# An edge-gated graph layer on one core: edge sums in pairs two to three steps late, the add one step early, products of a block spread over its steps

## The chip, the core and the metric

The kernel runs on one core of a Trainium2 chip. The metric is the device time of one execution in microseconds (us). A core has TensorE (PE, with its weight loads PEld), VectorE (DVE), ScalarE (ACT), GpSimd (POOL) and SyncE (SP), which run side by side, each through its own queue in order, and 16 DMA engines that all queues share.

## The reference

A layer of a graph network over B = 16 batches, N = 1024 nodes and D = 256 features. `adj` is sparse: some 9 of 1024 entries in a column are not zero, and A_a = A_m = adj.

```
pre_u = einsum('bud,dk->buk', h_t, W1[:d])
pre_v = einsum('bvd,dk->bvk', h_t, W1[d:])
hidden = relu(pre_u[:, :, None, :] + pre_v[:, None, :, :] + b1)
S = sigmoid(einsum('buvk,ko->buvo', hidden, W2)[..., 0] + b2[0])
a_t = einsum('buv,bud->bvd', S * A_a, h_t)
m_t = einsum('uv,bud->bvd', A_m, h_t) * h_t
z_t = beta1 * h_t + beta2 * (einsum('bvd,de->bve', a_t, Wa) + ba) + beta3 * (einsum('bvd,de->bve', m_t, Wm) + bm)
```

## The kernel before

**Edges, not pairs.** The kernel makes a list of edges per 128 columns v of `adj` (`lists`, L239 to 373): the rows u of the nonzero entries and their values. Only where there is an edge does it work out the gate S. Nodes with more edges than a list holds are finished in a loop at the end (L842 on), none of whose instructions shows in the trace.

**Tables.** Batches are taken in 4 groups of GB = 4. Per group there is a table in DRAM with 1024 rows of 8 KB: pre_u of 4 batches, then h of 4 batches. `rows` (L434) makes the first half of 128 rows with TensorE (`half_product`, L425 to 428), ScalarE copies it out (tile `tab`, L443), SP stores it (L446); `copy_h` (L419) copies the second half from DRAM to DRAM, issued on ACT's queue in the main loop.

**Blocks and steps.** A block is (group, 128 nodes v); there are 32, in an order that takes node blocks 0 to 5 of groups 0 and 1 first, since lists are still being made. A block has T = 10 steps: two windows (w) of 64 nodes, of TW = 5 steps, each of 128 edges. A step n = 10k + s does this:

- `fetch` (L494) has GpSimd gather the 128 table rows of the step's edges into one of NF = 6 buffers `fetched`, about 0.94 MB. It is issued for step n - 1 + 6 once step n - 1 has been summed. `fetch_val` (L379) gathers edge values of new lists, two per step.
- `expand` (L564) has TensorE copy pre_v of each edge's node to its row: `pc` = mark x X, 128 x 1024 in PSUM (two buffers, pool `psc`). X is made by `halves` (L452) for the block after this one: products with w_v (L427), b1 by L431, copies by ScalarE (L461 to 468) and a subtraction by VectorE (`low`, L463).
- `gate` (L598) has VectorE add `fetched` and `pc` into the one tile `t` (L601), then make relu, the product with W2 and its sum for each of 4 batches (L606); ScalarE makes the sigmoid (L609) and scales the edge values by it (L612) into tile `left`, which `left_adj` (L573) has filled with the edge values for each batch (L579).
- `aggregate` (L614) has TensorE sum the edges of a node (L623): the stationary operand is a 128 x 32 piece of `left` (16 nodes, once with and once without gate), so that 4 batches lie side by side in 128 columns, in a half of an accumulator `acc0` or `acc1`. A step touches one quarter of the window (8 instructions in the trace) or two (16).
- `half_end` (L628) has ScalarE copy an accumulator to `ev0` or `ev1` (L631) when half a window is complete.

**Products of a block.** `turn_over` (L633) transposes `ev` on TensorE (L641), copies it by ScalarE into `LT` (L644), and some steps later VectorE multiplies the ungated half by h (`times_h`, L654). `block_end` (L659) then makes, in four pieces, the products with Wa and Wm (L672) and the bias (L431), copies them to tile `z` by ScalarE (L675), adds beta1 x h on VectorE (L676; h in `h_blk`, loaded by SP at L775) and stores z through SP (L678). Transposes, products, rows and halves share two PSUM buffers named `misc` (pool `psm`).

**What sets the order.** The order on each engine is written by hand (`manual_schedule`, L471): instructions are queued as the Python loop at L745 calls them. `after(step, f)` puts f off to `do(step)`, which stands behind `gate` of that step. `fill` puts one VectorE instruction of a list under way ahead of each gate product. `plan` (L726) says at which steps a block's x is loaded (first number) and its row products are made. Per step the queue order is:

```python
        if 1 <= n <= total:
            aggregate(n - 1)
            fetch_val(2)
            if n - 1 + NF < total:
                fetch(n - 1 + NF)
        ...
            gate(n)
            if n + 1 < total:
                left_adj(n + 1)
        ...
        do(n)
        if n + 2 < total:
            expand(n + 2)
```

Behind these come the block's pieces: `turn_over` at s = 1 (last quarter pair of the block before), 7 (two) and 9, `block_end` at s = 3 to 6, `halves` at s = 0, 2, 3, 5, 6.

## Time and profile before

| | us |
|---|---|
| runs of the kernel | 1163.63, 1163.78, 1171.99 |
| their median | 1163.78 |
| the profiled execution, first to last instruction (span) | 1165.8 |
| PE busy | 1092.1 (94%) |
| PEld busy | 723.1 (62%) |
| DVE busy | 1056.2 (91%) |
| ACT busy | 893.5 (77%) |
| POOL busy | 439.9 (38%) |
| bytes moved by DMA | 391.40 MB, mean 336 GB/s |
| of these the gathers' queue | 300.50 MB, 68.9% of the 16 engines' span |

The profile is that of one execution. The time of the profiled execution is known as its span alone. Ends of matmuls are modelled, since they are pipelined: starts are what to read on TensorE. A matmul in fp32 shows as two records, one in fp32r as one. On VectorE a gate product shows as the product and a short DVE_READ_ACCUMULATOR. A share of DMA is the mean share of time in which its 16 engines had a packet under way; packets overlap a little, so that it can pass 1. "A <- B" in a list of waits says that A's engine stood idle until B ended. Block k starts where I put the add (L601) of its step 0: 71.6 us for block 0, 309.4 for block 6, 513.2 for block 12, 897.6 for block 24, 1117.5 for block 31.

### The profile page before, as it was taken

How to read it: one execution, taken by the hardware profiler on the slowest of the kernel's cores; microseconds unless marked ns; L12 is line 12 of the kernel's file. 1: busy time of each engine (PE TensorE's matmuls, PEld its weight loads, DVE VectorE, ACT ScalarE, POOL GpSimd, SP SyncE). 2: the span in 40 equal slices, each digit the busy share in tenths (PEclk: the TensorE clock that was granted, in tenths of full speed). 3: DMA queues.
4: the chain of work that ended last, by engine and by line, in shares of the span. 5: the costliest groups of instructions: out<-in, count | busy, mean ns of one | idle time of the engine just before them, and what ended most of it. 6: DMA issues, size and time to landing. Idle time of an engine off the chain costs nothing. (4 is left out here: it accounts for less than half of the span.)

```text
span 1165.8 us, 23918 instructions
## 1 busy us (share of the span) xinstructions
PE 1092.1 (94%) x7633; PEld 723.1 (62%) x7633; DVE 1056.2 (91%) x3487; ACT 893.5 (77%) x2624; POOL 439.9 (38%) x428
## 2 busy tenths in 40 slices
PE   7867899999999999999999999999999999999986
PEld 6744666666666666666666666666666666666553
DVE  7688889888999989999999999999999999999994
ACT  2346587767887878888888888888888888888873
POOL 1556645253335333443333333333333333333330
PEclk9868899999999999999999999999999999999999
DMA  9986898999999999999999999999998998999991
GB/s 286 298 307 223 277 372 312 362 320 331 342 320 323 396 379 336 358 350 402 389 374 369 355 364 356 360 364 383 371 375 324 361 322 333 334 339 328 328 346 60
DMA packets 147048, 391.40 MB, mean 336 GB/s; under 512 B 16753, under 2 KB 105329, under 8 KB 110705
## 3 DMA queue, kind: packets, MB, share of 16 engines
q0 software_dynamic: 50016, 300.50, 68.9%
q1 hardware_dynamic: 81616, 74.99, 20.0%
q10 hardware_dynamic: 15280, 14.29, 3.7%
q8 instruction: 63, 1.03, 0.3%
q14 instruction: 73, 0.59, 0.1%
HBM read 393.78 MB, written 50.33 MB: 381 GB/s over the span
## 5 line engine op out<-in xcount | busy, mean ns | idle before, releaser
L496 POOL DMA_INDIRECT fetched<-table,uidx x320 | 341.5, 1067 | 628.3 <-PE acc L623 447.2
L606 DVE SCALAR_TENSOR_TENSOR t<-t,w_b 128x256 f32<-128x256 f32 x1280 | 478.3, 421 | 19.3 <-ACT left L612 0.5
L601 DVE TENSOR_TENSOR t<-fetched,pc 128x1024 f32<-128x1024 f32 x320 | 389.3, 1217 | 41.4 <-PE pc L569 13.9
L623 PE MATMUL acc<-fetched,left 128*32 128x256 f32 x4096 | 336.2, 391 | 31.9 <-ACT left L612 26.2
L612 ACT ACTIVATE left<-left,gt 128x32 f32<-128x32 f32 (+1 forms) x1280 | 299.3, 304 | 10.4
L569 PE MATMUL pc<-X,mark 128*128 128x512 f32 x640 | 237.6, 453 | 6.2 <-ACT mark L562 5.0
L623 PEld LDWEIGHTS acc<-fetched,left 128*32 128x32 f32 x4096 | 130.6, 109 | 179.3 <-issue 52.4
L569 PEld LDWEIGHTS pc<-X,mark 128*128 128x128 f32 x640 | 97.2, 191 | 140.0 <-issue 89.3
L609 ACT ACTIVATE gt<-sc,b_b 128x4 f32<-128x4 f32 x320 | 96.2, 301 | 43.4 <-DVE t L606 40.8
L672 PE MATMUL misc<-w_m,LT 128*128 128x256 f32 x496 | 117.2, 379 | 0.0
L672 PE MATMUL misc<-w_a,LT 128*128 128x256 f32 x496 | 117.1, 379 | 0.0
L579 ACT ACTIVATE left<-onehot,val 128x128 f32<-128x128 bf16 (+1 forms) x320 | 116.5, 364 | 0.0
L427 PE MATMUL misc<-w_v,hT 128*128 128x256 f32 x448 | 107.3, 383 | 0.0
L427 PE MATMUL misc<-w_u,hT 128*128 128x256 f32 x416 | 101.2, 390 | 5.7 <-ACT few L329 3.6
L606 DVE DVE_READ_ACCUMULATOR t<-t,w_b 128x1 f32 x1280 | 104.0, 81 | 0.0
L672 PEld LDWEIGHTS misc<-w_a,LT 128*128 128x128 f32 x496 | 93.9, 189 | 15.1
L672 PEld LDWEIGHTS misc<-w_m,LT 128*128 128x128 f32 x496 | 93.8, 189 | 14.9
L382 POOL DMA_INDIRECT val<-in_adjT_dram,vidx x80 | 85.7, 1071 | 35.1 <-issue 22.4
L427 PEld LDWEIGHTS misc<-w_v,hT 128*128 128x128 f32 x448 | 86.0, 192 | 13.9
L427 PEld LDWEIGHTS misc<-w_u,hT 128*128 128x128 f32 x416 | 79.5, 195 | 17.3 <-ACT few L329 3.7
L631 ACT COPY ev<-acc 128x512 f32<-128x512 f32 x128 | 75.5, 590 | 14.6 <-PE acc L623 4.2
L675 ACT COPY z<-misc 128x512 f32<-128x512 f32 x62 | 36.3, 586 | 58.1 <-PE misc L672 38.8
(164 smaller groups left out, 947.9 us busy)
## 6 DMA issues: line engine op xcount, KB each, us to landing
h_blk<-in_x_dram SPq DMA_DIRECT2D x31, 512.0 KB
out_dram<-z SPq DMA_DIRECT2D x31, 512.0 KB
hT<-in_xT_dram SPq DMA_DIRECT2D x28, 512.0 KB
table<-in_x_dram ACTq DMA_DIRECT2D x24, 512.0 KB
table<-tab SPq DMA_DIRECT2D x24, 512.0 KB
fetched<-table,uidx POOLq DMA_INDIRECT x320
table<-in_x_dram SPq DMA_DIRECT2D x8, 512.0 KB
table<-fetched SPq DMA_DIRECT2D x8, 512.0 KB
```

The costliest lines, as they stand in the source:

```text
L382: nc.gpsimd.indirect_dma_start(out=val[:, i, j:j + 1], out_offset=None, in_=adj_flat, in_offset=bass.IndirectOffsetOnAxis(ap=vidx[:, i, j: ...
L427: nc.tensor.matmul(p[:, bb * D:(bb + 1) * D], hT[:, 2 * h + bb, i, :], wt[:, i, :], start=(i == 0 and not begun), stop=(i == DC - 1), skip ...
L496: nc.gpsimd.indirect_dma_start(out=fetched[n % NF], out_offset=None, in_=table[g], in_offset=bass.IndirectOffsetOnAxis(ap=uidx[:, vt * NW ...
L569: nc.tensor.matmul(pcs[n][:, c], marks[n // TW][:, j * P:(j + 1) * P], cuts[k][:, w, c], start=True, stop=True)
L579: nc.scalar.activation(lefts[n][:, :m, :, 0, :], onehot[:, i, o:o + m, :].unsqueeze(2).to_broadcast([P, m, GB, V]), AF.Copy, scale=val[:, ...
L601: nc.vector.tensor_tensor(t, fetched[n % NF][:, :GD].rearrange("p (b d) -> p b d", b=GB), pcs.pop(n).rearrange("p (b d) -> p b d", b=GB), ...
L606: nc.vector.scalar_tensor_tensor(t[:, b, :], t[:, b, :], 0.0, w2_b, ALU.max, ALU.mult, accum_out=sc[:, b:b + 1])
L609: nc.scalar.activation(gt, sc, AF.Sigmoid, bias=b2_b)
L612: nc.scalar.activation(lefts[n][:, :m, b, 1, :], lefts[n][:, :m, b, 0, :], AF.Copy, scale=gt[:, b:b + 1])
L623: nc.tensor.matmul(accs[h][b * 2 * V:(b + 1) * 2 * V, r, :], left[:, i, b].rearrange("p k v -> p (k v)"), f[:, GD + b * D:GD + (b + 1) * D ...
L631: nc.scalar.copy(evs[q], accs.pop(q))
L672: nc.tensor.matmul(pz[:, bb * D:(bb + 1) * D], LTs[k][:, c, 2 * h + bb, i, :], wt[:, c, :], start=False, stop=(i == 0 and c == DC - 1), sk ...
```

## The change

- **Add one step ahead, in place.** `gate` is cut in two: `add(n)` puts fetched + pc into the gathered buffer itself (no tile `t`), and is called for step n + 1 ahead of `gate(n)`.
- **Edge sums in pairs.** `aggregate` is called at odd n alone, for steps n - 3 and n - 2, and in order at the very end. `left` has five buffers in place of three. It holds the ungated values once for two batches (7 slots of 16 in place of 8), so ScalarE's first copy into it is half as large.
- **Gather buffers.** 7 in place of 6, freed in order of use (`free`, `at_slot`), and an eighth from step 110, when the lists are done and their pool `lst` is closed. Gathers are issued as buffers come free, two at a time.
- **z without a tile of its own.** ScalarE copies the product into `LT`, whose transposed sums are used up; VectorE adds beta1 x h into `h_blk`, and the store leaves from `h_blk`. `LT` is laid out anew, and the transposes write `pt` in runs of 16.
- **Products spread.** `turn_over` at s = 0, 2, 8, 9; row products by new plans (groups 2 and 3 at s = 8 and 9, the last at step 219 where it was 233). Up to step 119 expand and products are queued ahead of the step's add and gate, from 120 on behind them as before.

```diff
+    lst = lst.enter_context(tc.tile_pool(name="lst", bufs=1))
...
-    NF = 6
+    NF = 7
+    at_slot, free = {}, list(range(NF))
...
     def fetch(n):
         k, g, vt, w, j = where(n)
+        at_slot[n] = free.pop(0)
         nc.gpsimd.indirect_dma_start(
-            out=fetched[n % NF], out_offset=None, in_=table[g],
+            out=fetched[at_slot[n]], out_offset=None, in_=table[g],
...
-        lefts[n] = wk.tile([P, 2, GB, 2, V], FP, name="left")
-        nc.scalar.activation(lefts[n][:, :m, :, 0, :], onehot[:, i, o:o + m, :].unsqueeze(2).to_broadcast([P, m, GB, V]),
+        lefts[n] = wk.tile([P, 2, 2 * GB - 1, V], FP, name="left", bufs=5)
+        nc.scalar.activation(lefts[n][:, :m, 1::GB, :],
+                             onehot[:, i, o:o + m, :].unsqueeze(2).to_broadcast([P, m, GB // 2, V]),
                              AF.Copy, scale=val[:, i, j:j + 1])
...
+    def add(n):
+        t = fetched[at_slot[n]][:, :GD]
+        nc.vector.tensor_tensor(t, t, pcs.pop(n), ALU.add)
+
     def gate(n):
-        k, g, vt, w, j = where(n)
-        t = one.tile([P, GB, D], FP, name="t")
-        nc.vector.tensor_tensor(t, fetched[n % NF][:, :GD].rearrange("p (b d) -> p b d", b=GB),
-                                pcs.pop(n).rearrange("p (b d) -> p b d", b=GB), ALU.add)
+        m = len(QUARTERS[n % TW])
+        t = fetched[at_slot[n]][:, :GD].rearrange("p (b d) -> p b d", b=GB)
...
-                                 left[:, i, b].rearrange("p k v -> p (k v)"), f[:, GD + b * D:GD + (b + 1) * D],
+                                 left[:, i, 2 * b - b % 2:2 * b - b % 2 + 2].rearrange("p k v -> p (k v)"), f[:, GD + b * D:GD + (b + 1) * D],
...
-            LTs[k] = one.tile([P, DC, GB, 2, P], FP, name="LT")
+            LTs[k] = one.tile([P, GB, 2, DC, P], FP, name="LT")
         LT = LTs[k]
-        pt = small("pt")
+        pt = small("pt").rearrange("p (r k c v) -> p r k c v", r=2, c=DC, v=V)
...
-            nc.tensor.transpose(pt[:, i * P:(i + 1) * P], ev[:, r, c * P:(c + 1) * P], ident)
+            nc.tensor.transpose(pt[:, r, :, c, :], ev[:, r, c * P:(c + 1) * P], ident)
...
-        after(step + (1 if k == BS - 1 else 2), times_h)
+        after(step + (1 if k == BS - 1 or w else 2), times_h)
...
-            nc.scalar.copy(z[:, sl], pz.rearrange("p (b d) -> p b d", b=2))
-            after(step + 2, lambda sl=sl: nc.vector.scalar_tensor_tensor(z[:, sl], hb[:, sl], be1, z[:, sl],
-                                                                         ALU.mult, ALU.add))
-        after(step + 3, lambda: nc.sync.dma_start(
-            out[g * GB:(g + 1) * GB, vt * P:(vt + 1) * P, :].rearrange("b p d -> p b d"), z))
+            z = LTs[k][:, 2 * h].rearrange("p k c n -> p (k c n)").rearrange("p (b d) -> p b d", b=2)
+            nc.scalar.copy(z, pz.rearrange("p (b d) -> p b d", b=2))
+            after(step + 1, lambda sl=sl, z=z: nc.vector.scalar_tensor_tensor(hb[:, sl], hb[:, sl], be1, z,
+                                                                              ALU.mult, ALU.add))
+        after(step + 2, lambda: nc.sync.dma_start(
+            out[g * GB:(g + 1) * GB, vt * P:(vt + 1) * P, :].rearrange("b p d -> p b d"), hb))
...
+    def products(n, k, s):
+        nonlocal end, parts, piece, last
+        if (s == 2 and 0 < k < BS) or n == total:
             turn_over(k - 1, 1, 1, n)
...
+        if s in (8, 9) and n < total - T:
+            turn_over(k, 0, s - 8, n)
...
+        if (s == 0 and 0 < k < BS) or n == total - 1:
+            turn_over(k - (s == 0), 1, 0, n)
...
+    ROOM, MORE = 110, 1
+    ahead = NF
+    add(0)
+
+    def refill():
+        nonlocal ahead
+        while free and ahead < total:
+            fetch(ahead)
+            ahead += 1
+
+    def gather_in(n):
+        aggregate(n)
+        free.append(at_slot.pop(n))
+        fetch_val(2)
+        refill()
+        if (n + 1) % TW in (0, MID + 1):
+            half_end(n, 0 if (n + 1) % TW else 1)
+
+    done = 0
+    for n in range(total + 2):
+        k, s = divmod(n, T)
+        if n < total - 3:
+            last_in = n - 1 if n % 2 else done
+        else:
+            last_in = n
+        while done < min(last_in, total):
+            gather_in(done)
+            done += 1
...
+        if n < 120:
+            if n + 2 < total:
+                expand(n + 2)
+            products(n, k, s)
+        if n + 1 < total:
+            add(n + 1)
+        if n < total:
+            gate(n)
+            if n + 1 < total:
+                left_adj(n + 1)
+        do(n)
+        if n >= 120 and n + 2 < total:
+            expand(n + 2)
...
+        if n >= 120:
+            products(n, k, s)
+        if n == ROOM:
+            assert not running and all(next(x, None) is None for x in made)
+            lists_done()
+            more = main.enter_context(tc.tile_pool(name="more", bufs=1))
+            for i in range(MORE):
+                free.append(len(fetched))
+                fetched.append(more.tile([P, 2 * GD], FP, name=f"fetched{len(fetched)}"))
+            refill()
```

## The prediction

> **What bounds the kernel now.** I read the view by stretches first, cut at the start of blocks 0, 6, 12, 24 and 31 (ten steps each, the last from 1117.5 us). Columns: stretch, its length, busy us of TensorE, weight loads, VectorE, ScalarE and GpSimd, granted clock, share of the DMA engines, GB/s.
>
> ```profile
> 71.00:309.00 238.00, 216.90 (x1423) 143.50 (x1422) 205.30 (x706) 168.93 (x492) 117.20 (x114) 0.94 0.89 312
> 309.00:513.00 204.00, 197.20 (x1400) 130.92 (x1401) 194.21 (x649) 165.08 (x487) 86.51 (x81) 1.00 0.96 352
> 513.00:898.00 385.00, 382.72 (x2767) 252.32 (x2766) 363.83 (x1145) 325.96 (x973) 131.25 (x122) 1.00 0.99 368
> 898.00:1117.00 219.00, 212.04 (x1529) 134.65 (x1527) 210.08 (x665) 184.73 (x557) 72.77 (x70) 1.00 0.92 335
> ```
>
> Three resources are close to full at once: TensorE 99%, VectorE 95% and DMA 0.99 from 513 to 898; VectorE 96% with DMA down to 0.92 afterwards. A share says little then; the timeline must show who never stands still. First VectorE in block 27, where no table rows are made any more:
>
> ```profile
> 1000.40 0.08 DVE L606 DVE_READ_ACCUMULATOR t<-t,w_b 128x1 f32 x1
> 1000.57 1.22 DVE L601 TENSOR_TENSOR t<-fetched,pc 128x1024 f32<-128x1024 f32 x1
> 1001.89 0.42 DVE L606 SCALAR_TENSOR_TENSOR t<-t,w_b 128x256 f32<-128x256 f32 x1
> ...
> 1003.28 0.69 DVE L654 TENSOR_TENSOR LT<-LT,hT 128x512 f32<-128x512 f32 x1
> 1003.88 1.21 DVE L601 TENSOR_TENSOR t<-fetched,pc 128x1024 f32<-128x1024 f32 x1
> 1005.13 0.42 DVE L606 SCALAR_TENSOR_TENSOR t<-t,w_b 128x256 f32<-128x256 f32 x1
> ```
>
> No other engine is waited for, yet VectorE loses time. The add starts 0.09 after the last gate instruction ends (1000.48 to 1000.57), and the first gate instruction starts 0.10 after the add ends (1001.79 to 1001.89): each needs what the one before it did to tile `t`. Where an unrelated instruction stands between (L654), add and product overlap by 0.08 (1003.97 against 1003.88). So a block is bound here by VectorE's own neighbours. It takes 31.29 us (add to add, 991.99 to 1023.28), and so does nearly every block from 24 to 30. Now TensorE in block 21:
>
> ```profile
> 801.35 1.07 PE L623 MATMUL acc<-fetched,left 128*32 128x256 f32 x16
> 802.35 0.73 PE L569 MATMUL pc<-X,mark 128*128 128x512 f32 x2
> 802.92 0.60 PE L641 MATMUL misc<-ident,ev 128*128 128x128 f32 x4
> 803.45 0.64 PE L623 MATMUL acc<-fetched,left 128*32 128x256 f32 x8
> 804.01 0.72 PE L569 MATMUL pc<-X,mark 128*128 128x512 f32 x2
> 804.58 0.39 PE L431 MATMUL misc<-b_p,unit 128*128 128x512 f32 x1
> 804.81 1.89 PE L427 MATMUL misc<-w_v,hT 128*128 128x256 f32 x8
> 806.63 0.64 PE L623 MATMUL acc<-fetched,left 128*32 128x256 f32 x8
> ```
>
> Each group starts before the one ahead of it ends; the starts are back to back through blocks 20 and 21, 31.3 us each. So up to 898 TensorE is full too, and switching has a price in it. A full-width record costs 0.216 (1.89 less the last one's 0.379, over 7), so the 8 of L427 need 1.73; the edge sums follow after 1.82: 0.09 to enter. Edge sums of 8 records take 0.57 (803.45 to 804.01), of 16 take 1.00: 0.43 per 8 and 0.14 once. The first `pc` record behind them takes 0.335 (0.73 less 0.39), where a like one takes 0.23 (804.58 to 804.81): 0.105 more. Together 0.34 per visit, ten visits a block. Last, the waits (total, times, longest):
>
> ```profile
> POOL fetched L496 <- PE acc L623: 447.2, 204, 6.3
> DVE t L601 <- PE pc L569: 13.9, 18, 2.0
> ```
>
> GpSimd mostly waits for an edge sum to free a gather buffer: the gathers run as far ahead as six buffers let them. From the trace's semaphore updates a gather lands 7.1 us after its issue in blocks 0 to 11, 7.4 in 12 to 23 (nine in ten within 9.4) and 6.0 later, and has 9.9 us on average before its add in blocks 12 to 23.
>
> **The change, part by part.**
> *Add one step ahead.* Nothing is removed; in the built order add(n+1) stands in front of the four gate instructions of step n, so no two neighbours touch one tile. I price every border like the one at L654, overlap 0.08. Of ten steps five have an instruction between (two L654, two L676, one L463) and five have none: 5 x (0.09+0.08 + 0.10+0.08) + 5 x (0.03+0.08) = 2.3. A block of VectorE falls from 31.29 to 28.9. The add now heads the queue: if its gather or `pc` is late, the gates of the step before stand behind it, then ScalarE's gate values. The bounds are 2.3 and 0.
>
> [...] The row at L654 shows a negative gap, so the sum goes by the row.
>
> *Edge sums in pairs, two to three steps behind.* Five visits fewer: 5 x 0.34 = 1.7 of TensorE per block, 31.3 to 29.6 with rows; without rows (16 records of 0.216, 3.5) about 26. Their wait for ScalarE's `left` (50.7 + 26.2 in the whole list of waits, 7.5 + 3.5 of it from 1000 to 1100) goes as well. Late next are the two `misc` buffers: transposes and products at s = 8, 9, 0 each need ScalarE to have copied the tile two before, which stands behind the gate of that step. Laid out with VectorE's starts, TensorE waits about 0.6 a block.
>
> *Gather buffers.* Six become seven, eight from step 110, but each is held from the add to an edge sum three steps later, and two gathers are issued together (1.07 each on GpSimd, behind four value gathers of 1.07 where lists are new). With step time T, the first of a pair is held 3T, 1.4 of ScalarE (0.30 the gate, 0.96 the four scalings, borders), 1.6 of edge sums and 1.1 of issue; so it has 4T - 4.1 to land with seven buffers and 5T - 4.1 with eight. At T = 3.1 that is 8.3 and 11.4, against 7.1 and 7.4 on average. Its cover shrinks in blocks 0 to 10; with eight it holds, if TensorE is not late. I charge about 1 us a block up to step 110 and 0.7 in blocks 12 to 23, where DMA at 0.99 would have to move the same bytes in 30.9 us. It can: 8 KB packets took 0.309 at best and 0.347 on average.
>
> *z into the used-up LT, LT turned round.* The tile z goes, its copy (L675, 62 x 586) and sum (L676, 62 x 747) stay; the product (L654) has the same 512 elements. The output leaves from `h_blk`, so SP's next load of `h_blk`, two steps later, waits for that store to land, and the xT load and table store queue behind it. They are needed five to eight steps (15 us) later: nothing. ScalarE's first copy into `left` halves (0.387 to 0.33, a 64-element row): 0.4 a block off an engine at 84%, nothing. The transposes now write runs of 16 elements. No row shows a strided one on TensorE; ScalarE's L644 writes such runs at 574 ns against 586 to 590 for plain copies. Bounds 0 and doubling, 16 x 0.109 = 1.7 a block; I take 0 by that row.
>
> *Products spread; rows earlier.* Same instructions; the last row piece moves from step 233 to 219, so block 23 (33.7 us, 2.5 of VectorE waits, GpSimd waiting for a table store) loses a stall.
>
> **Sum.** 898 to 1117: seven blocks from 31.4 to about 29.4 (28.9 plus 0.5 of `misc`), 14. 513 to 898: twelve from 32.0 to 30.9 (29.6 + 0.6 + 0.7), 13. 309 to 513: six blocks, list work already fills half the borders; 1.8 less 1.0 each, 5. 71 to 309: 1.2 each, 7. Tail 2, head 0. That is 41 off a span of 1165.8, 1124.8. The profiled execution stands 2.0 above the median of the runs, 1163.78; so 1123 us.
>
> **Rivals.**
> *Both floors reached.* Gathers stay hidden; blocks fall to 30.0 (12 to 23) and 29.0 (24 to 30): 24 + 17, and 13 + 11 + 3 elsewhere, 68, so 1096. For it: idle waits of VectorE are small now. Against: DMA at 0.99.
> *Transposes double or stalls eat the early gain.* TensorE keeps 31.3 in blocks 0 to 23; what is left is 14 + 2, less 5 of stalls before step 110: 1153.
> *Slower: gathers with seven buffers.* Steps 0 to 109 take (480.8 - 71.6)/110 = 3.72 us, so the first of a pair has 10.8 to land. If pairs behind value gathers raise the landing, T = (L + 4.1)/4. The later gain of 29 is eaten at 0.26 us a step, T = 3.98, L = 11.8; that is the deciding point, 4.7 above the mean seen. At L = 12.7, T = 4.2: 110 x 0.48 = 53, less 29: 1188. For it: landings up to 15.6 in block 0; against it: nine in ten are within 9.4.
> That the change does not do what it says is excluded by the built order.
>
> **How the numbers follow.** Forecast 0.62 (its own range 1106 to 1140), floors 0.15, doubled transposes 0.14, slower 0.09. A measurement of this kernel tells about 1% from no change, 1152 to 1175. The third case straddles 1152, half to each side: faster 0.62 + 0.15 + 0.07 = 0.84, same 0.07, slower 0.09. The range, 1096 to 1156, leaves out the slower case and half of the floors, 0.16.
>
> **What would show it.** Borders of VectorE negative throughout and blocks 24 to 30 near 29.4; 16 to 32 records of edge sums in one group, five groups a block, with TensorE's starts still back to back in blocks 12 to 22; the add's waits for gathers, 2.8 us now, at some tens of us at most, in blocks 0 to 10; transposes still 0.109 apart. Wrong would be: blocks 24 to 30 still at 31.3 (borders stay), transposes 0.2 apart, or the add waiting over 100 us for gathers.

## The result, and the profile after

The changed kernel took 1232.62 us (median of four runs, 1225.38 to 1243.85) where the kernel before took 1164.57 beside it: a ratio of 1.0526, 95% interval 1.0458 to 1.0594. The ratio goes by the fast runs alone, and the one at 1243.85 was slow, so that it is not the quotient of the two medians. The forecast was 1123, its range 1096 to 1156. The change made the kernel 5% slower. The profiled execution of the changed kernel has a span of 1226.1, that of the kernel before 1165.8.

The view by stretches, cut at the starts of the same blocks as before (0, 6, 12, 24, 31), with the same columns: stretch, length, busy us of TensorE, weight loads, VectorE, ScalarE and GpSimd, granted clock, DMA share, GB/s.

```profile
69.00:307.00 238.00, 207.00 (x1409) 142.69 (x1407) 198.00 (x698) 163.40 (x484) 120.59 (x113) 0.91 0.89 311
307.00:527.00 220.00, 197.52 (x1415) 137.03 (x1413) 188.52 (x649) 162.38 (x492) 87.95 (x81) 0.94 0.93 328
527.00:960.00 433.00, 380.65 (x2763) 265.66 (x2760) 349.42 (x1142) 318.88 (x969) 128.24 (x122) 0.92 0.89 329
960.00:1176.00 216.00, 201.96 (x1519) 136.18 (x1513) 202.72 (x668) 179.57 (x553) 75.51 (x71) 0.96 0.93 336
```

From add to add, blocks 24 to 30 went from 219.9 us to 215.8, blocks 12 to 23 from 384.4 to 433.3, blocks 6 to 11 from 203.8 to 220.0, blocks 0 to 5 from 237.8 to 237.5: of the 60 us lost, 49 lie in blocks 12 to 23 and 16 in blocks 6 to 11. In the long stretch DMA fell from 0.99 to 0.89 and TensorE from 99% to 88%: nothing is full any more, so the engines wait for one another. The clock, 1.00 before, is 0.92. Block by block: 13 to 22, in all of which row products run, take 34.6 to 40.6 us, and in each of them one add is 6.7 to 12.7 us behind the one before it (s = 0 to 1). Block 23, without rows, takes 29.7 at once.

VectorE in block 27, the lines that answer to those of the kernel before (start, us, instruction):

```profile
1036.77 0.69 DVE L663 TENSOR_TENSOR LT<-LT,hT__6925 128x512 f32<-128x512 f32 x1
1037.37 1.21 DVE L606 TENSOR_TENSOR fetched<-fetched,pc 128x1024 f32<-128x1024 f32 x1
1038.50 0.42 DVE L614 SCALAR_TENSOR_TENSOR fetched<-fetched,w_b 128x256 f32<-128x256 f32 x1
```

The add starts 0.09 before L663 ends, and the first gate product 0.08 before the add ends. The borders are negative, as the forecast had it; a step without an extra instruction is 2.51 us (it was 2.8 to 2.9). That part is right, and not what was decisive.

The waits (us in all, times, longest), then SP's alone from 528 to 930 us:

```profile
POOL fetched L501 <- PE acc L631: 571.4, 142, 14.2
DVE fetched L606 <- PE pc L574: 120.4, 45, 10.1
...
PE misc L431 <- DMA hT<-in_xT_dram: 35.1, 7, 8.2
```

```profile
SPq L450 <- ACT gt L617: 143.1, 11, 14.9
SPq L687 <- DMA h_blk<-in_x_dram: 95.7, 10, 12.6
SPq L687 <- DVE h_blk L685: 62.5, 7, 13.2
...
SPq L855 <- DMA out_dram<-h_blk: 6.7, 1, 6.7
```

VectorE's add now waits 120 us for `pc` (13.9 before), TensorE's row products wait for the xT load, and SP stands 143 us in front of the table store (86 in blocks 12 to 23 of the kernel before). Followed back from the last instruction, the chain of work that ended last goes from 560 to 900 us through xT loads for 69% of the time, one behind the other with a row product between (start, us, what):

```profile
653.20 24.53 DMA hT__6925<-in_xT_dram
677.87 3.46 PE misc L431 x8
687.79 26.73 DMA hT<-in_xT_dram
714.65 3.75 PE misc L431 x8
```

That is a circle: each load waits for something that the load before it released. One turn of it, SP's queue first and then TensorE:

```profile
652.05 0.34 SPq L450 DMA_DIRECT2D table<-tab  x1
652.48 0.67 SPq L855 DMA_DIRECT2D h_blk<-in_x_dram  x1
653.20 1.14 SPq L420 DMA_DIRECT2D hT__6925<-in_xT_dram  x1
674.77 0.38 SPq L687 DMA_DIRECT2D out_dram<-h_blk  x1
686.80 0.34 SPq L450 DMA_DIRECT2D table<-tab  x1
687.23 0.51 SPq L855 DMA_DIRECT2D h_blk<-in_x_dram  x1
687.79 0.99 SPq L420 DMA_DIRECT2D hT<-in_xT_dram  x1
```

```profile
674.17 0.60 PE L649 MATMUL misc<-ident,ev 128*128 128x128 f32 x4
677.87 3.46 PE L431 MATMUL misc<-w_u,hT__6925 128*128 128x256 f32 x8 [3.10 <-DMA hT__6925<-in_xT_dram]
681.26 2.07 PE L631 MATMUL acc<-fetched,left 128*32 128x256 f32 x32
683.25 0.73 PE L574 MATMUL pc<-X,mark 128*128 128x512 f32 x2
...
684.25 1.89 PE L431 MATMUL misc<-w_u,hT__6925 128*128 128x256 f32 x8
```

The xT load issued at 653.20 lets the row products go at 677.87, 24.7 us later. TensorE had stood 3.10; the edge sums and the next `pc` stand behind the rows, and VectorE's add waits 4.30 for that `pc` (684.08). The second row product comes at 684.25, ScalarE's copy at 686.18, the table store at 686.80, and right behind it in SP's queue the next xT load, at 687.79. From load to load 34.6 us: 24.7 of landing and 9.9 of path back. Block 16 takes 34.8; the next two turns, 37.5 and 34.4, stand beside blocks of 37.3 and 34.6. So the turn of the circle is the period of a block, whatever the engines could do. The row product took 3.46 where the like one at 684.25 took 1.89: the granted clock was 0.5 from 678.17 to 681.58, after the stand.

The kernel before has the same order in SP's queue in blocks 19 to 22, and no stall:

```profile
738.07 0.34 SPq L446 DMA_DIRECT2D table<-tab  x1
738.50 0.39 SPq L775 DMA_DIRECT2D h_blk<-in_x_dram  x1
738.98 0.97 SPq L416 DMA_DIRECT2D hT<-in_xT_dram  x1
```

```profile
776.16 1.89 PE L427 MATMUL misc<-w_u,hT 128*128 128x256 f32 x8
```

There the first row product that needs this load starts 37.2 us behind its issue, and 33 to 40 us behind for the others whose rows are made in blocks 12 to 23. The change plans it eight steps behind the load, and it comes after 24.7 us, at once when the load has landed. The store ahead of the loads closes the circle only together with that short lead.

### The profile page after: what moved, and what is told of

The parts are those of the page before. It is cut to its first block, busy times and chain, and to the rows that moved or that the text cites. A ratio compares the mean times of both kernels' runs of the same rounds, so it can differ in the third digit from the quotient of the medians.

```text
span 1226.1 us, 23758 instructions
## 1 busy us (share of the span) xinstructions
PE 1067.3 (87%) x7633; PEld 741.7 (60%) x7633; DVE 1021.5 (83%) x3487; ACT 874.4 (71%) x2624; POOL 444.6 (36%) x428
## 4 chain that ended last, share of the span: by engine, by line
DMA 28%; DVE 28%; PE 26%; issue 11%; ACT 4%; POOL 1%; ACTq 0%; SPq 0%; POOLq 0%; DVEq 0%
DMA hT<-in_xT_dram 15%; DVE fetched L614 13%; PE misc L431 11%; DVE fetched L606 9%; PE acc L631 6%; DMA fetched<-table,uidx 5%; PE pc L574 3%; PE misc L680 2%; DMA hT__6552<-in_xT_dram 2%; DMA hT__6925<-in_xT_dram 2%; DMA h_blk<-in_x_dram 2%; PE misc L649 1%; DVE low L467 1%; ACT left L619 1%; DMA val<-in_adjT_dram,vidx 1%
## 5 line engine op out<-in xcount | busy, mean ns | idle before, releaser
L606 DVE TENSOR_TENSOR fetched<-fetched,pc 128x1024 f32<-128x1024 f32 x320 | 388.2, 1213 | 158.9 <-PE pc L574 120.4
L614 DVE SCALAR_TENSOR_TENSOR fetched<-fetched,w_b 128x256 f32<-128x256 f32 x1280 | 475.0, 417 | 0.0
L631 PE MATMUL acc<-fetched,left 128*32 128x256 f32 x4096 | 278.1, 395 | 4.7 <-ACT left L619 2.2
L574 PEld LDWEIGHTS pc<-X,mark 128*128 128x128 f32 x640 | 107.6, 192 | 109.7 <-DVE fetched L606 38.3
L431 PE MATMUL misc<-w_u,hT 128*128 128x256 f32 x416 | 120.4, 444 | 52.8 <-DMA hT<-in_xT_dram 35.1
L431 PEld LDWEIGHTS misc<-w_u,hT 128*128 128x128 f32 x416 | 88.9, 222 | 69.6 <-ACT LT L652 21.1
L431 PE MATMUL misc<-w_v,hT 128*128 128x256 f32 x448 | 118.6, 412 | 0.0
L584 ACT ACTIVATE left<-onehot,val 128x64 f32<-128x64 bf16 (+1 forms) x320 | 102.9, 321 | 0.0
L614 DVE DVE_READ_ACCUMULATOR fetched<-fetched,w_b 128x1 f32 x1280 | 101.1, 79 | 0.0
L649 PE MATMUL misc<-ident,ev 128*128 128x128 f32 x512 | 81.4, 282 | 17.8 <-ACT ev L639 10.2
```

The lines of the kernel that those rows point to most:

```text
L431: nc.tensor.matmul(p[:, bb * D:(bb + 1) * D], hT[:, 2 * h + bb, i, :], wt[:, i, :], start=(i == 0 and not begun), stop=(i == DC - 1), skip ...
L574: nc.tensor.matmul(pcs[n][:, c], marks[n // TW][:, j * P:(j + 1) * P], cuts[k][:, w, c], start=True, stop=True)
L584: nc.scalar.activation(lefts[n][:, :m, 1::GB, :], onehot[:, i, o:o + m, :].unsqueeze(2).to_broadcast([P, m, GB // 2, V]), AF.Copy, scale=v ...
L606: nc.vector.tensor_tensor(t, t, pcs.pop(n), ALU.add)
L614: nc.vector.scalar_tensor_tensor(t[:, b, :], t[:, b, :], 0.0, w2_b, ALU.max, ALU.mult, accum_out=sc[:, b:b + 1])
L631: nc.tensor.matmul(accs[h][b * 2 * V:(b + 1) * 2 * V, r, :], left[:, i, 2 * b - b % 2:2 * b - b % 2 + 2].rearrange("p k v -> p (k v)"), f[ ...
```

## The experiments

Theory 1 is this circle. Rival 2 is the TensorE clock by itself: it would halve because edge sums in pairs leave TensorE more holes. Rival 3 is that the DMA engines cannot carry gathers in pairs beside the traffic of the rows. Times stand beside runs of the kernel before on the same chip: 1173.2 for the first four experiments, 1149.5 to 1150.1 for the others, so ratios are compared, with their 95% intervals.

**The load earlier**

```diff
-        plan([(g, vt) for vt in range(NT)], ((first + 10 * i, first + 8 + 10 * i, first + 9 + 10 * i)
+        plan([(g, vt) for vt in range(NT)], ((first + 10 * i - 3, first + 8 + 10 * i, first + 9 + 10 * i)
...
```

> The xT load of groups 2 and 3 (and the copy of h into the table that goes with it) is issued three steps earlier, at s = 7 of the block before, so ahead of the output store, the table store and the load of h_blk in SP's queue. Theory 1 (a loop through SP: row products late, so the table store late, so the next xT load behind it late, so the next row products late): xT lands before s = 8, TensorE no longer stands for it, blocks 13 to 22 fall from a mean of 37 us to 31 to 32.5, the clock stays at 1.0 there, and the time is about 1170 us (1155 to 1185). Rival 2 (the TensorE clock, which halves because TensorE has more holes since the edge sums come in pairs, is the cause by itself): the holes stay, 1215 to 1232. Rival 3 (the DMA engines, at 0.99 before, do not stand gathers in pairs beside row traffic): the bytes are the same, 1215 to 1232.

1182.73 us, ratio 1.0109 (1.0046 to 1.0171). Blocks 13 to 22 average 31.8, most at 30.4 to 31.6. Same bytes, same edge sums, so rivals 2 and 3 fall as main causes. What is left are steps of 6.6 to 9.3 us at s = 6 of blocks 12, 14 and 16 (3.2 to 4.4 elsewhere), where VectorE waits for `h_blk`.

**The table store later**

```diff
-        after(step + 1, lambda: nc.sync.dma_start(table[g][nt * P:(nt + 1) * P, :GD], tab))
+        after(step + (3 if g > 1 else 1), lambda: nc.sync.dma_start(table[g][nt * P:(nt + 1) * P, :GD], tab))
```

> The table store of groups 2 and 3 is put off by two steps, so that the h_blk load and the xT load stand ahead of it in SP's queue; nothing else moves. Theory 1: the loop is cut at the store, but the xT load still stands behind the h_blk load, which waits for the output store to land (7 to 8.5 us after s = 8), so it is issued at about s = 1 and lands at s = 8 or 9: blocks 13 to 22 at 33 to 35 us, time 1185 to 1210. If the loop through the table store were no part of it: 37 us a block, 1220 to 1235. Rivals 2 and 3: no change, 1220 to 1235.

One run at 1179.88 us and three at 1199.76 to 1200.73: too far apart for a ratio. The profile is of the one at 1200.73 and has blocks 13 to 22 at 34.1, as theory 1 had it, with the circle through the store cut but only eight steps for the load to land. Since the fastest run has no profile, this experiment decides nothing by itself.

**The h_blk load later**

```diff
-        if s == 0 and 0 < k < BS:
+        if s == 2 and 0 < k < BS:
```

> The load of h_blk is moved from s = 0 to s = 2, behind the xT load; the table store stays ahead of the xT load. It prices by itself what the shared tile (the output store leaves from h_blk, so that its next load waits for the store to land) does to the xT load. If that wait is the deciding link of the loop: blocks 13 to 22 at 32 to 33 us, 1175 to 1190. If the table store is the deciding link: 36 to 37 us, 1215 to 1230; the list of waits then shows SP waiting for the table's copy as before. Rivals 2 and 3: 1220 to 1235.

1293.75 us, ratio 1.1059 (1.0991 to 1.1126): none of the forecasts. VectorE now stands for `h_blk`: the step at s = 6 takes 12 to 18 us in ten blocks. The run does not tell the links apart, but it shows that `h_blk` had no slack either.

**Rows from a resident x** (the table's rows of groups 2 and 3 are then not those of the layer)

```diff
-        half_product(p, hTs[k], w_u, h, False)
+        half_product(p, hTs[k if g < 2 else order[step // T]], w_u, h, False)
```

> The row products of groups 2 and 3 multiply the x of the block under way, which has long been in its buffer, in place of the x just loaded: that part of the computation is changed. Every instruction, load and store stays and keeps its place; only the wait of the row products for the load is gone. Theory 1: the same gain as a load in time, blocks 13 to 22 at 31 to 32.5 us, about 1170 us (1155 to 1185), although the xT load still lands 20 us or more after its issue. Rival 2 (clock by itself): 1215 to 1232. Rival 3 (DMA engines): 1215 to 1232.

1201.81 us, ratio 1.0242 (1.0146 to 1.0338); blocks 13 to 22 at 32.8. Without the wait for xT the stall at s = 0 is gone, with all its traffic still there; stalls at s = 6 for `h_blk` (23.0 us in all) remain, since table store and loads kept their places.

**Two h_blk buffers on top of the earlier load**

```diff
-            hbs[k - 1] = big.tile([P, GB, D], FP, name="h_blk", bufs=1)
+            hbs[k - 1] = (more if n > 120 and k % 2 else big).tile([P, GB, D], FP, name="h_blk", bufs=1)
```

> e1_load_early with a second buffer for h_blk from step 120 on, so that the next load of h_blk no longer waits for the last output store to land. The stalls that e1 has left at s = 6 (blocks 12, 14, 16, 20, some 16 us in all, where VectorE waits for h_blk) are put down by theory 1 to that wait: they go, blocks 13 to 22 are at 30.4 to 31.5 us, and the time is 12 to 18 us below e1 on the same chip, about 1167 us beside a kernel before of 1170. Rival: the load of h_blk is late because the table store, or the gathers' packets, hold it up; then the stalls stay and the time is that of e1 within 5 us.

1164.9 us, ratio 1.0158 (1.0091 to 1.0225), not below the earlier load alone. Three stalls of 3.4 to 5 us at s = 6 remain in blocks 13 to 22, so it came out as the rival had it. In block 14 the load of `h_blk` was issued at 577.40, before the output store had landed (585.37 by its semaphore), and landed at 598.01 all the same: 20 us where 11.5 to 14 were seen in blocks 12 to 22 of the change. Two transfers that SP had issued ahead of it were still under way then, the output store and the table store (landed at 588.7). So this load, issued on time, landed late all the same.

**Earlier load and later store together**

```diff
+        after(step + (3 if g > 1 else 1), lambda: nc.sync.dma_start(table[g][nt * P:(nt + 1) * P, :GD], tab))
...
+        plan([(g, vt) for vt in range(NT)], ((first + 10 * i - 3, first + 8 + 10 * i, first + 9 + 10 * i)
...
```

> e1_load_early and e2_store_late together: the xT load ahead of the output store, the table store behind the load of h_blk, one h_blk buffer as in the change. If the wait of the h_blk load for the output store is what is left (theory 1), this is no better than e1 (within 6 us) and stalls at s = 6 stay; if the table store in front of the h_blk load is, the stalls go as in the run with two buffers, 12 to 18 us below e1.

1166.34 us, ratio 1.0169 (1.0112 to 1.0225): one run at 1144.48, which is 0.995 of the kernel before, and three from 1165 to 1176, to which the ratio fits. So by time it stays open whether the two moves are better than the earlier load alone. The profile is of the one at 1144.48 (span 1142.6); where the others lost their 21 us or more no trace shows. In the profile eight of the ten blocks 13 to 22 are at 30.4 to 30.7; block 13 stands 9 us for `h_blk`, whose load went out at 550.50, the moment the output store had landed (550.49; it was issued at 531.00). So the shared tile can count once the circle is cut; 30.4 is what a row block takes without a stall.

**Filling a hole of TensorE.** In the changed kernel's blocks without rows some take 29.65 and some 31.3. Four stretches of 3.41 us that follow each other in block 26:

```profile
1019.51:1022.92 3.41, 3.35 (x32) 1.88 (x24) 3.41 (x13) 2.78 (x12) 2.13 (x3) 1.00 0.96 320
1022.92:1026.33 3.41, 1.47 (x9) 0.93 (x8) 3.41 (x16) 2.71 (x10) 0.00 (x0) 1.00 1.00 418
1026.33:1029.75 3.42, 3.42 (x12) 2.16 (x14) 3.06 (x10) 2.14 (x8) 0.00 (x0) 0.50 1.03 426
1029.75:1033.16 3.41, 3.41 (x36) 2.36 (x29) 1.43 (x2) 2.83 (x8) 1.94 (x2) 1.00 0.63 190
```

TensorE was busy 1.47 of 3.41 (0.43), and ran the next stretch at half clock. It had waited 0.62 and 1.32 us for ScalarE, in a block where it has time to spare.

```diff
-        for h in range(2):
+        for h in (0, 1) * (2 if n >= 232 and n % T == 2 else 1):
             c = slice(2 * h * D, (2 * h + 2) * D)
             nc.tensor.matmul(pcs[n][:, c], ...
```

> e1_load_early, and in blocks 23 to 31 the two pc products issued at s = 0 are made twice over (same values; 0.43 us more TensorE work a block), in the hole that TensorE has there. If the clock is halved for a stretch of 3.41 us whenever TensorE was busy for less than about 0.46 of the stretch before (as a comparison of all stretches of the changed kernel's trace has it: 0.45 and less was followed by half clock, 0.47 and 0.49 not), the hole is filled to above that, no half-clock stretch is left in blocks 24 to 30, and all seven take 29.6 to 29.8 us where four or five of them took 31.3: 6 to 8 us off e1. If the halving has another cause, four or five blocks stay at 31.3, and the time stays within 3 us of e1.

1169.61 us, ratio 1.0137 (1.0063 to 1.021), against 1.0109 for the earlier load alone: the total shows no gain. Blocks 23 to 30 do: all are at 29.67 but for one (32.9, `h_blk` late at s = 6, its load held up by the output store), where five of seven took 31.3. The stretch with the hole now:

```profile
1031.76:1035.17 3.41, 1.93 (x10) 1.48 (x10) 3.41 (x12) 2.68 (x11) 0.00 (x0) 1.00 1.01 401
1035.17:1038.59 3.42, 3.42 (x33) 2.06 (x32) 2.69 (x11) 3.14 (x10) 0.99 (x1) 1.00 0.98 383
```

More work made these blocks shorter: 0.57 busy, and the next stretch keeps its clock.

**Products behind the gate from the start** (on the earlier load)

```diff
-        if n < 120:
+        if n < 0:
...
-        if n >= 120 and n + 2 < total:
+        if n + 2 < total:
...
-        if n >= 120:
+        if n >= 0:
             products(n, k, s)
```

> e1_load_early with expand and products queued behind the step's add and gate from step 0 on, as the kernel before has it, where the change queues them ahead up to step 119. Blocks 0 to 11 took 441.6 us before and 457.5 us after the change, 454.3 in e1. If the new place of the products (ScalarE's copies out of misc now stand ahead of the gate, and TensorE waits for them) makes those stalls, blocks 0 to 11 fall below 445 us and the time by 10 us or more. If the later edge sums and the add standing ahead of the gates make them, it is no better: blocks 0 to 11 at 450 to 470 us, the time within 10 us of e1 or worse.

1192.7 us, ratio 1.0376 (1.0338 to 1.0415), worse by 2% than the three runs beside it (1164.9 to 1169.6); blocks 0 to 11 at 463.8. The new place of the products is a gain, not the cause.

**All four repairs** (the earlier load, with these)

```diff
+        after(step + (3 if g > 1 else 1), lambda: nc.sync.dma_start(table[g][nt * P:(nt + 1) * P, :GD], tab))
...
+            hbs[k - 1] = (more if n > 120 and k % 2 else big).tile([P, GB, D], FP, name="h_blk", bufs=1)
...
+        for h in (0, 1) * (2 if n >= 232 and n % T == 2 else 1):
```

> The change with all four repairs: xT loads three steps earlier, table stores two steps later, a second h_blk buffer from step 120, and the pc products at s = 0 made twice in blocks 23 to 31. The profile of the run with the first two moves showed 30.44 us for a row block without a stall and 29.67 for a block without rows and without half clock. Theory 1: all of blocks 14 to 22 at 30.4 to 31, blocks 23 to 30 at 29.7, 15 to 20 us below e6_both_moves, so 1.5 to 2.5 per cent faster than the kernel before on the same chip. Rival (the remaining stalls at s = 6 come from the DMA engines' load and not from the order in SP's queue): three or more row blocks stay at 33 us and more, and it is level with the kernel before within 1 per cent.

1145.4 us, ratio 0.9968 (0.9942 to 0.9993). Blocks 14 to 22 at 30.5 to 30.7 but for one (32.8), 23 to 30 at 29.7: theory 1 in blocks 12 to 30. The total misses its 1.5 to 2.5 per cent by what blocks 0 to 11 still take, 441 us.

**Single edge sums**

```diff
-            last_in = n - 1 if n % 2 else done
+            last_in = n - 1
```

> e9_all_moves with the edge sums undone from pairs: at every step the one of two steps before, ten visits of TensorE a block in place of five. The prediction priced the five visits at 1.7 us a block on TensorE's path in blocks with rows: then blocks 14 to 22 go from 30.4 to 31.3 or a little more, and the time up by 10 us or more. If TensorE is not the bound there, the row blocks stay at 30.4 and the time stays, or falls, since gathers are then issued one at a time and earlier.

1150.24 us, ratio 1.0032 (1.001 to 1.0055). Four row blocks with single sums, then four with pairs (run before):

```profile
672.40:798.00 125.60, 125.60 (x930) 82.30 (x929) 117.04 (x383) 106.93 (x324) 45.79 (x40) 1.00 1.00 378
```

```profile
701.80:823.90 122.10, 120.86 (x932) 85.24 (x928) 116.21 (x381) 105.77 (x324) 43.45 (x40) 1.00 1.01 386
```

The time rose by 5 us, not by 10. With single sums TensorE is full, 31.4 a block; pairs bring 30.5. So five visits are worth 0.9 a block, not 1.7 (TensorE's busy time falls by 1.2, part of which it then waits). In blocks without rows single sums, two steps behind, are the better ones: 29.4 against 29.67.

**The add one step ahead, alone, in the kernel before**

```diff
...
+        if n + 1 < total:
+            add(n + 1)
         if n < total:
             gate(n)
```

> The kernel before with one part of the change alone: the add in place in the gathered buffer and one step ahead. The prediction put 2.3 us a block on it, since no border of VectorE is then between two instructions on one tile: blocks 24 to 30 at 28.9 to 29.7 us where they take 31.3, a step of add and gates alone at 2.51 us, and 12 to 17 us off the stretch of these seven blocks. Gathers have one step less to land (6.9 us on average where they had 9.9; they take 6 to 7.4), so that stalls for gathers may take some of it back in blocks 0 to 23, where TensorE at 31.3 a block holds in any case. In all 10 to 20 us faster than the kernel before, or level if the gathers come late.

1176.13 us, ratio 1.0256 (1.0224 to 1.0287). VectorE's borders are gone, and blocks 24 to 30 take 31.3, as before; the waits moved (whole run):

```profile
DVE fetched L600 <- PE pc L569: 86.1, 111, 7.1
PEld acc L625 <- ACT left L614: 70.1, 137, 7.0
```

Of these, 11.8 and 14.4 us lie between 902 and 1120 us. TensorE still takes the sums of the step just gated, waits for ScalarE's `left`, and the next `pc` stands behind that. Alone, this part of the change brings nothing in these blocks and loses elsewhere. With the other parts they take 29.4 (the run before this one); that it is the later sums among them that free it is argued from the waits, not tried apart.

**Single sums in the first 118 steps** (on all four repairs)

```diff
-            last_in = n - 1 if n % 2 else done
+            last_in = n - 1 if n % 2 or n < 118 else done
```

> e9_all_moves with single edge sums in steps 0 to 117 alone, where the kernel has seven buffers and list work: buffers come free sooner and one at a time. If the pairs with seven buffers are what made blocks 0 to 11 16 us longer after the change (441.6 to 457.5), they fall by 10 us or more against e9 on the same chip. If it is the holes of TensorE and ScalarE's queue (list copies and DMA issues in front of misc copies), they stay within 5 us of e9's, or grow by the 0.34 us a visit.

1145.8 us, ratio 0.9964 (0.9941 to 0.9986); blocks 0 to 11 at 440.3, as with pairs. Waits of the add for gathers fell from 28.3 to 9.6 us there and the time stayed: pairs with seven buffers are not what costs most in these blocks.

**Rows of group 1 apart.** In those blocks ScalarE stood 11.8 us for tile `tab`. With all four repairs, SP's store and then ScalarE's two copies:

```profile
182.26 0.34 SPq L450 DMA_DIRECT2D table<-tab  x1
```

```profile
181.65 0.58 ACT L447 COPY tab<-misc 128x512 f32<-128x512 f32 x1
...
191.87 0.58 ACT L447 COPY tab<-misc 128x512 f32<-128x512 f32 x1 [5.94 <-DMA table<-tab]
```

The copy for the next rows waits until the store of the last ones has landed; there is one `tab`, and the new plan makes rows at steps 28 and 29, 47 and 48.

```diff
-    plan(turn[NT:], ((0, 5, 7), (6, 11, 14), (12, 18, 19), (17, 27, 28), (24, 29, 31), (31, 37, 38), (38, 44, 47),
+    plan(turn[NT:], ((0, 5, 7), (6, 11, 14), (12, 18, 19), (17, 27, 28), (24, 31, 34), (31, 37, 38), (38, 44, 45),
...
```

> e9_all_moves with two row products of group 1 moved apart: the second of (24, 29, 31) to 34, and 47 of (38, 44, 47) to 45, so that the table store between two sets of rows has three steps to land in place of one. In e9's profile ScalarE stood 11.8 us in blocks 0 to 11 for the store of tile tab, in two waits of 5.9, with TensorE's products and the add behind it. If that is a main part of the loss in blocks 0 to 11: 8 to 14 us less there than in e9 (441 us), and the time 6 to 14 us lower on the same chip. If the waits only cover others, those blocks stay within 4 us.

1133.77 us, ratio 0.9867 (0.9843 to 0.9891); no wait for `tab` is left, blocks 0 to 11 at 428.7.

**The version that the runs point to** (rows apart, all repairs but the doubled `pc`)

```diff
-            last_in = n - 1 if n % 2 else done
+            last_in = n - 1 if n % 2 or n < 118 or n >= 232 else done
```

> The version that the runs point to: loads, stores, two h_blk buffers and rows apart as in e13, edge sums in pairs only in steps 118 to 231 (where rows are made and TensorE is the bound) and single ones elsewhere, without the doubled pc products. From the runs: blocks 14 to 22 at 30.5, blocks 23 to 30 at 29.4 without half clock (e10), blocks 0 to 11 as in e13 or a little less, since gathers come free one at a time. Against e13 2 to 6 us less; against the kernel before on the same chip 1 to 2 per cent faster.

1129.42 us, ratio 0.9829 (0.9808 to 0.9851). Blocks 0 to 11 at 426.0, 24 to 30 at 29.4.

**The marks stored by SP**

```diff
-                (nc.gpsimd if vt < EARLY else nc.scalar).dma_start(whose[h * W:(h + 1) * W, vt * NW + w, :], few[w * W:(w + 1) * W])
+                (nc.gpsimd if vt < EARLY else nc.sync).dma_start(whose[h * W:(h + 1) * W, vt * NW + w, :], few[w * W:(w + 1) * W])
```

> e14_mixed with the four stores of a list's marks (whose) issued by SP in place of ScalarE, four times from step 20 on. In e9 ScalarE's copy of the list product stood behind these issues and TensorE's next product waited for it, 8 us in three waits; the trace of the kernel before shows 2.7. If this counts: 4 to 8 us less in blocks 0 to 11 than e14. If SP is then late with its own stores and loads, or the waits lie beside others: within 3 us of e14, or more.

1121.45 us, ratio 0.976 (0.9732 to 0.9787): the fastest, 2.4% below the kernel before. Blocks 0 to 11 at 422.0, 4 us less; the other 4 us lie elsewhere. Its stretches, cut at blocks 0, 6, 12, 23 and 31:

```profile
72.00:290.00 218.00, 203.40 (x1402) 135.09 (x1400) 197.61 (x698) 162.94 (x484) 119.76 (x112) 0.97 0.95 341
290.00:494.00 204.00, 195.99 (x1396) 130.05 (x1396) 188.54 (x647) 161.15 (x486) 87.85 (x81) 1.00 0.98 350
494.00:835.00 341.00, 333.86 (x2573) 234.93 (x2575) 319.86 (x1047) 291.82 (x895) 119.43 (x113) 0.99 1.01 386
835.00:1072.00 237.00, 228.11 (x1739) 144.75 (x1731) 232.45 (x763) 205.75 (x632) 91.44 (x81) 1.00 0.94 352
```

DMA is back at 1.01 in the long stretch and moves 386 GB/s, more than the 368 before the change, with pairs beside the rows: rival 3 is excluded.

**The kernel before, on this chip**

> The kernel before, unchanged, for its profile on the same chip as the three others. If the chip makes no difference to the stages: blocks 0 to 11 at 441.6 us, 12 to 22 at 350.7, 23 to 30 at 253.6, as in the first profile. If the chip is a faster one, the difference lies in blocks 0 to 22, where DMA is at 0.89 to 0.99, and blocks 24 to 30 stay at 31.3.

1153.57 us, 1.0037 times its seven other runs beside it (1.0005 to 1.0068), which shows what a ratio near 1 is worth. Blocks 0 to 11 take 431.0 here (441.6 in the first profile), 12 to 22 take 348.9 (350.7), 24 to 30 again 31.3. So in these two profiles the repaired change is faster in each stretch on one chip: 422.0 against 431.0, 341 against 349, 237 against 253. Of the first difference see below: single profiles of like code differ by more in blocks 0 to 11.

**The sharing undone, alone, in the change as it is** (the two h_blk buffers)

> The change as it is, with a second h_blk buffer from step 120 on and nothing else moved: the next load of h_blk no longer waits for the output store to land. In the profile of the change SP stood 143 us before the table store in blocks 12 to 22 and only 6.7 us before the load of h_blk for the output store. If the table store's place is the cause (theory 1): the loop stays, blocks 13 to 22 at 35 to 37.5 us, the ratio to the kernel before at 1.04 to 1.055, as the change itself (1.0526). If the sharing is the cause: blocks 13 to 22 at 32 us or less, ratio below 1.02.

1227.24 us, ratio 1.0653 (1.0606 to 1.0701); blocks 13 to 22 at 37.3.

```profile
DVE fetched L606 <- PE pc L574: 124.5, 47, 10.0
PE misc L431 <- DMA hT<-in_xT_dram: 45.2, 8, 8.4
```

The circle stays whole. The shared tile did not make it; the load's short lead, with the store's place ahead of the loads, did.

## Why the prediction was wrong, by its steps

*z into LT, and the xT load behind it.* This is the step that failed: "They are needed five to eight steps (15 us) later: nothing." The load's need was not compared with its landing. Eight steps at the forecast's own 30.9 a block are 24.7 us; the loads of blocks 15 to 17 took 23.1 to 25.7 us from the end of their issue to their last semaphore update. At that pace the load has no slack even if SP issues it at once. It was as slow in the kernel before (18.3 to 26.1 us in the five loads there whose updates are all in the trace), but had 33 to 40 us. The wait that the step named, the `h_blk` load behind the output store, held SP for 6.7 us in blocks 12 to 23, and undoing it alone left the circle whole (1.0653); with the circle cut it cost 9 us in one block of one profile.

Why so long, as far as the packets show it: the load comes in 512 KB of 512-byte packets, 1024 in all, 64 for each of the 16 engines if they are spread evenly. The one issued at 725.28 has its first packet at 731.18, behind all 128 of the table store and 288 of the 512 of `h_blk`, and its last at 749.0. From 737 to 742 us, 242 of its packets and 237 of the gathers' start: on average one for one. In the trace such a packet takes 0.027 us and a gather's 8 KB packet 0.309 (medians). If each of the 64 waits for one of the gathers', that is 64 x 0.336 = 21.5, an estimate from these rows; 17.8 were seen from the first to the last. In the us from 736 on, with 30 gather packets where the five later ones have 45 to 49, 248 of its own start. What orders the packets of an engine the trace does not tell.

*Products spread; rows earlier.* "Same instructions" was true, and the step still failed: the new plan has the rows eight steps, some 25 us, behind their load's issue where they had 33 to 40 us, with the table store directly ahead of both loads, and closed the circle; and in group 1 it put two sets of rows around one `tab`. Moving load and store by three and two steps gives 30.4 to 30.7 a row block; the forecast was 30.9, near by luck: the visits saved 0.9 in place of 1.7, and next to none of the 1.3 charged for waits was paid. Block 23 lost its stall, as forecast.

*Add one step ahead.* Size right, reason half right: 31.3 fell to 29.4 with later sums and no half clock, to 29.65 with pairs, against a forecast 29.4. But the statement that a block is bound here by VectorE's own neighbours fell: without the borders alone it stays at 31.3. The prediction's own view had TensorE at 212.04 of 219 us there, 97%, against VectorE's 96%. (31.29 less 2.3 is also 29.0, not 28.9.) The row at L654 held for the borders: where VectorE waits for nothing, the add and the gate product behind it start 0.07 to 0.09 before the instruction ahead of them ends, throughout blocks 24 to 30. And the prediction's sign of being wrong, blocks at 31.3, came in five of seven blocks with the borders gone: from the clock, as follows.

*Edge sums in pairs.* The term of 1.7 measured 0.9. The waits of TensorE for two `misc` buffers were foreseen (0.6 a block; 0.62 and 1.32 in block 26); that half clock follows them was not: in the change 42 stretches begun between 70 and 1110 us, 143 us, ran at half clock, 6 (20 us) before. How much of the 60 us this alone costs was not separated in row blocks, where it follows the stalls; in blocks 24 to 30 it is 1.6 a block, in five of seven.

*Gather buffers.* Landings in blocks 12 to 22 averaged 6.8 to 8.4 us, around the 7.4 charged; the add's waits for gathers are 22.8 us in blocks 0 to 11 (some tens at most, as forecast), and with single sums 9.6 without a gain. The slower rival, gathers, is not what happened.

*Transposes.* They start 0.109 apart: nothing, as taken.

Blocks 0 to 11 were forecast 12 us shorter and came out 16 longer, all of it in blocks 6 to 11 (203.8 to 220.0). There three profiles with the earlier load as the one edit that bears on them have 204.4 to 212.6; the change again (in the run with two `h_blk` buffers, which come later) has 225.1, and the run with a resident x 218.2. So the load's place in SP's queue has a share, but not through the row products' wait for xT, which the resident x takes away. The rest stays open. Three other edits took blocks 0 to 11 from 441 to 422 on like chips, in one profile each: rows around one `tab` (12), single sums (3), list stores issued by ScalarE (4). The first of them gained 10 in blocks 0 to 5, which the change had not lengthened, and the kernel before stood 11.8 us for `tab` in its second profile too. Single profiles of like code differ by 13 us in blocks 0 to 11 (438 and 452 in two runs on one chip); what bears the edits out is the time of the runs, 1145.4, 1133.8, 1129.4 and 1121.5, though part of the last two steps lies elsewhere.

## What to carry to other kernels

When an edit moves a load or a store, write down two things for each DMA. One is its landing time, as the trace has it, beside the time until its first use at the forecast's own pace. The other is the list of what stands ahead of it in its queue, and what that waits for: if a load's first use leads back to what stands ahead of the next load, there is a circle, and once it has no slack its length is the period (here 34.6 us from load to load, beside 34.8 for the block). Try each part of a change alone, since another engine may be as busy as the one that it unburdens: here the add a step ahead alone left a block at 31.3. And read the granted clock by short stretches: here holes of 0.62 and 1.32 us were followed by 3.41 us at half clock.

## What the runs showed of the hardware

In the trace of the change the granted TensorE clock is 1.0 or 0.5, and all its changes lie multiples of 3.413 us apart. In the change all 21 full-clock stretches of that length between 70 and 1110 us with TensorE busy for 0.45 of it or less were followed by one at 0.5; of the seven between 0.47 and 0.65 two were (0.57 and 0.64), and one at 0.77 was too. Ends of matmuls are modelled, so the bound is not sharper than that. Nor were these stretches all idle: the one shown above, with 1.47 us of work and no gap over 1.32, was followed by half clock.

Small packets beside large ones: in blocks 12 to 22 of the change 512 KB of x landed 18 to 29 us after the end of its issue in 512-byte packets, and 11.5 to 14 us after it in `h_blk`'s 1 KB packets (20 once, in the run with two buffers), while 0.94 MB gathered in 8 KB packets took 6.8 to 8.4 us on average of a block.
